# Reordering the end of layer 0's aggregation in a four-layer graph network: tail rows, T1's subtractions and one sum of quarters

## The chip, the cores and the metric

The kernel runs on one core of one Trainium2 chip. The metric is the device time of one execution in microseconds. Besides the timed runs there is one profiled execution, whose trace gives every instruction with its start, its length, its engine and what released it. All positions in the text below ("at 263.54") are microseconds from the start of that trace.

## The reference

`x` is 2708 x 512, `adj` is 2708 x 2708, all in float32. Four layers follow each other; each adds its result to `x`:

```
h = relu(layernorm(x))                                   # before every layer
layer 0: x += relu( dinv * ((adj + I) @ (dinv * h)) @ W0 )     # deg = adj.sum(1), dinv = (deg + 1) ** -0.5
layer 1: x += (dis * (adj @ (dis * h))) @ W1.T + b1            # dis = (deg + 1e-8) ** -0.5
layer 2: the form of layer 0 with W2
layer 3: x += sigmoid(attn_a * (softmax-like attention @ (h @ W_sa)) + attn_b * (adj @ (h @ W_g) + b_g))
```

In each layer the large piece is a product of `adj` (2708 x 2708) with 512 columns. The change concerns that product in layer 0 alone.

## The kernel before, in words

**Tiling.** The 2708 nodes are four quarters of 677. Of each quarter 640 rows (5 blocks of 128) go through the fast scheme below; the remaining 37 rows of each quarter are gathered in two "tail" row blocks (`NF` and `NF + 1`). The output of a product is kept transposed in `agg[128, 2, 2, 2, 2, 678]`: partition = feature within a block of 128, then half of the features, half of the output nodes, block in the half, quarter in the half, and the 677 columns of a quarter (one of padding), worked on in two halves `u` of 339 columns.

**Two levels of Strassen's scheme (Winograd's form).** A product is done as seven outer products (numbers 1 to 7) of sums of parts of `h` (`XA` to `XD`, formed in place in `h`) with sums of quarters of the adjacency (plain ones `y11`, `y12`, `y21`, `y22`, and sums `T1` to `T4`, kept in DRAM as `osum`). Each outer product is done for `u = 0` and `1`, and each of these is again seven inner products on TensorE: `inner_x` (L445) forms four sums of the features on VectorE, `inner_y` (L461) four sums of the four blocks `o11, o12, o21, o22` of the adjacency on VectorE (`t1` L468, `t2` L469, `t4` L470, `t3` L471, each 128 x 1695), and `multiply` (L486) runs the seven inner products in the fixed order `pa` (operand 1), `pb` (6, needs `t2`), `pa` again (2), `pc` (7, needs `t3`), `pd` (5, needs `t1`), `pc` again (4, needs `t4`), `pd` again (3). An inner product is 5 matmuls of 128 x 339 (10 records in the trace). The second use of a bank continues its sum, so VectorE must have read the first one: `u2` (L528) after `pb`, `u3` (L534) after `pc`, the writes to `agg` (L511 to L515) after `pd` and after the second `pc` and `pd`.

**Tail rows.** `tails` (L574) adds the 37-row remainders: for each quarter `q` and each `u` four matmuls over block `NF` (L549) and four short ones over `NF + 1` (L554), into four PSUM banks `pt`, of which three come from the same pool of five banks as `pa` to `pd`; each `pt` is added to `agg` by VectorE (L589). Their operand is loaded by `tail_rows` (L558): two transfers of 339 KB from `yt` on SyncE's queue, and two small VectorE additions for the self loops (L571).

**Order around the change.** In layer 0 `first_aggregate` (L629) runs the outer products 1 and 7 and then, for `u = 1` and then `u = 0`, the products 6, 2 and 4; then the tail rows of quarters 0 and 1; product 5 for `u = 0`, `1`; the tail rows of quarters 2 and 3; the epilogue of the first half of the nodes, `epilogue(H1)` (`next_x`, L832: projection `po` L822, relu on ScalarE L842, addition to `x` L847, layer norm); product 3; `epilogue(H2)`. In the iteration with `u = 0`:

- `t2u` holds the four blocks of T2. T4 = T2 + `y21` is formed into four other blocks (L767) and stored by GpSimd's queue; T1 = T2 - `y22` is formed in place, one block `k` at a time, by `third_less` (L770, subtraction at L775), each after a load of a block of `y22` on SyncE's queue into one of two buffers. These same two buffers then take the tail rows of quarters 0 and 1.
- The second half of T1 (`u = 1`) is made by transfers: `accumulated` (L662) loads `y12` on SyncE's queue and lets GpSimd's queue add `y11` to it during a transfer; then it is stored for later layers.
- `ends_of_sums` (L599) adds quarters of `agg` on VectorE: L600 adds `agg[:, 0, 1]` to `agg[:, 1, 1]`, L601 then adds `agg[:, 1, 1]` to `agg[:, 1, 0]`, 128 x 2712 each.
- `XB -= XD` (L784) and `XC += XA` (L794), 128 x 2560 each, prepare the products 5 and 3.

**Who orders the work.** Each engine executes its own queue. Where an instruction stands in it is decided when the program is built, by a scheduler with priorities from the order of the source; `with tc.issue_after(ins):` only places the instructions of its block behind `ins` in the queue of `ins`'s engine. `at_u2`, `at_u3`, `at_end` and the like are lists of instructions to refer to. Waits on data, buffers and banks are set automatically. An instruction that waits holds up everything behind it in its queue.

Of the kernel before, what the change touches and what calls it, by code (L numbers as in the profile page):

```python
# [1 line left out]

# [8 lines left out]
ALU = mybir.AluOpType  # L11
# [26 lines left out]
def gnn_kernel(  # L38
# [20 lines left out]
    nc = tc.nc  # L59
# [51 lines left out]
    agg = big.tile([P, 2, 2, 2, 2, U * W], FP, name="agg")  # L111
# [328 lines left out]
        nc.vector.scalar_tensor_tensor(o, a, -1.0, b, ALU.mult, ALU.subtract)  # L440


    at_v, at_u2, at_u3, at_end, at_shift = [], [], [], [], []

    def inner_x(X):  # L445
        n = half // 2
# [14 lines left out]
    def inner_y(blks, u, loops, t3=None):  # L461
        o11, o12, o21, o22 = blks
        if loops:
            add_loops(o11, u, loops)
            add_loops(o22, u, loops)
        t1, t2, t4 = (tpool.tile([P, KT, W], FP, tag="t", name=f"t{k}") for k in (1, 2, 4))
        t3 = o12 if t3 is None else t3
        nc.vector.tensor_add(t1, o12, o11)  # L468
        nc.vector.tensor_add(t2, o22, t1)  # L469
        nc.vector.tensor_add(t4, o21, t2)  # L470
        nc.vector.tensor_add(t3, o22, o12)  # L471
        return {1: o11, 2: o21, 3: o22, 4: t4, 5: t1, 6: t2, 7: t3}

    def outer_product(p, self_loops, *dests):
        X, key, times = OUTER[p]
        xs_ = inner_x(X)
        if key in PLAIN:
            loops = times if self_loops else 0
        else:
            loops = 0 if self_loops else -times  # L480
        for u in range(U):
            blks = [load_o(key, a, b, u) for a, b in QUAD]
            multiply(xs_, inner_y(blks, u, loops), u, dests)
            free.extend(blks)

    def multiply(xs_, ys, u, dests, beside=None):  # L486
# [4 lines left out]
        def product(ps, q, start):  # L491

            for k in range(KT):
                nc.tensor.matmul(  # L494
                    ps, xs_[q][:, k, :], ys[q][:, k, :],
                    start=start and k == 0, stop=k == KT - 1, skip_group_check=not start,
                )

        def bank(name):
            return ps_agg.tile([P, W], FP, tag="agg", name=name)  # L500
# [72 lines left out]

    def tails(self_loops, qs, loaded=None):  # L574

        for q in qs:
            blk, both = loaded[q] if loaded else tail_rows(self_loops, q)
            for u in range(U):
                tl = both[:, :, u]
                ps = [  # L580
                    (ps_agg if c < NC - 1 else ps_out).tile(
                        [P, W], FP, tag="agg" if c < NC - 1 else "out", name="pt"
                    )
                    for c in range(NC)
                ]
                tail_products(ps, tl, True)
                for c in range(NC):
                    d = agg[:, c // 2, q // 2, c % 2, q % 2, u * W : (u + 1) * W]
                    at_end.append(nc.vector.tensor_add(d, d, ps[c]).ins)  # L589
            free.append(blk)  # L590
# [38 lines left out]
    def first_aggregate(epilogue):  # L629
# [10 lines left out]
        t3 = {0: early[:2]}  # L640
# [32 lines left out]
        def keep_all(blks, key, u, a_b=QUAD):  # L673
            for a, b in a_b:
                keep_o(blks[QUAD.index((a, b))], key, a, b, u)


        t3 = {0: [free.pop(0), free.pop(0)] + t3[0], 1: blks[0]}
        came = {}
# [56 lines left out]
        for u in reversed(range(U)):  # L736
# [9 lines left out]
                    keep_all(t2u, "t2", u)  # L746
            multiply(xs_, ys, u, [(0, 1, "added")])
            u3_of_6 = at_u3[-1]
            if u == 1:
                with tc.issue_after(at_u2[-1]):  # L750
                    other_roots()
# [18 lines left out]
            def third_less(k, y, at):  # L770
                a, b = QUAD[k]
                if k > 0:
                    load_plain("y22", a, b, u, y)
                with tc.issue_after(at):
                    nc.vector.tensor_sub(t2u[k], t2u[k], y)  # L775

            if u == 1:
                free += [f for f in y21 if f is not early[2]]
                came = second_sums(QUAD[2:3])
            else:  # L780
                third_less(0, y22[0], at_u3[-1])
                third_less(2, y22[0], at_end[-1])
                with tc.issue_after(at_end[-1]):
                    nc.vector.tensor_sub(XB, XB, XD)  # L784
            xs_ = inner_x(XD)
            multiply(xs_, inner_y(t4, u, 0, own_t3), u, [(1, 0, "as it is")])
            if u == 1:
                free += t4
        third_less(1, y22[1], at_u2[-1])
        third_less(3, y22[1], at_end[-2])  # L790
        free += y22
        with tc.issue_after(at_end[-1]):
            rows = [tail_rows(True, q) for q in (0, 1)]
            nc.vector.tensor_add(XC, XC, XA)  # L794
        tails(True, (0, 1), rows)
        t1 = [t2u, [t4[3], more[2]] + [free.pop() for _ in range(2)][::-1]]
        assert not free
        came = accumulated({QUAD[k]: t1[1][k] for k in (0, 1, 3, 2)}, "y12", 1, "y11")
        ends_of_sums()
        xs_ = inner_x(XB)  # L800
        p5 = [(0, 1, "less"), (1, 1, "less")]
        for u in range(U):
            more_loops = OUTER[5][2] - (OUTER[6][2] if u == 0 else 0)
            if u == 1:
                with tc.issue_after(came):
                    keep_all(t1[u], "t1", u, QUAD[1:3])
            with tc.issue_after(at_end[-3]):
                ys = inner_y(t1[u], u, more_loops, own_t3 if u == 0 else None)
            keep_all(t1[u], "t1", u, QUAD if u == 0 else QUAD[::3])
            multiply(xs_, ys, u, p5)  # L810
        free += t2u + [f for f in t1[1] if f is not more[2]]
        tails(True, (2, 3))
        epilogue(H1)
        outer_product(3, True, (0, 1, "added"))
        epilogue(H2)


# [388 lines left out]
```

## Time and profile before

| | |
|---|---|
| median of 3 runs | 2152.69 us (2149.81 to 2153.11) |
| the profiled execution: its own time | 2146.91 us |
| its span in the trace | 2144.9 us (2.0 us lie around it) |
| TensorE matmuls busy | 2071.7 us of the span |
| VectorE busy | 1418.1 us |
| products 6, 2, 4 with `u = 0`: product 4's first matmul | at 250.19 |
| tails of quarters 0 and 1, first and last matmul | 258.75 to 297.2 |
| product 5, first to last matmul | 298.41 to 356.56 |
| tails of quarters 2 and 3 end, first matmul of `po` | 370.16 |
| epilogue H1 ends, product 3 begins | 404.60 |

The page has totals and 40 slices of the span; the other views are answers to questions about the trace: the timeline of an engine (start, length, engine, line, operation, what it writes and reads, count of records merged into the row, and in brackets the idle time ahead of it with what ended it), the busy time of the engines in given stretches, the waits, and the transfers with their time from issue to landing. Matmul ends in the trace are modelled and lie some 0.16 us after the start of the next.

### The profile page before, as it was taken

The numbers are of one execution on the slowest core, as the hardware profiler recorded it, in microseconds if no ns is written. First come the engines' busy times: TensorE is split into PE (matmuls) and PEld (weight loads), VectorE is DVE, ScalarE is ACT, GpSimd is POOL, SyncE is SP. The second block draws the span as 40 slices with busy tenths as digits, with TensorE's granted clock in tenths as the row PEclk, the third lists the DMA queues.
The fourth block names the chain that finished last, engine by engine and source line by source line (L and its number), as shares of the span: only waits on it lengthen the run. The fifth ranks groups of instructions, "written<-read, shape, count | busy, mean of one in ns | idle before, by whom it ended". The sixth has DMA issues, their size and how long they took to land.

```text
span 2144.9 us, 20028 instructions
## 1 busy us (share of the span) xinstructions
PE 2071.7 (97%) x7320; PEld 1289.3 (60%) x7320; DVE 1418.1 (66%) x2487; ACT 406.7 (19%) x826; POOL 180.9 (8%) x327
## 2 busy tenths in 40 slices
PE   5999988999999999999999999999999999999998
PEld 2566545556666645566664546666677666666664
DVE  3578857567676867776585969968537755666512
ACT  1330000221000010100002121000116534444401
POOL 0111010210000021100001130000001000000001
PEclk9999999999999999999999999999999999999999
DMA  9998484446554443654454556445541233233212
GB/s 370 295 363 254 165 271 172 164 142 207 177 172 162 156 163 132 230 177 157 164 171 138 202 191 218 169 156 159 189 168 71 96 101 106 88 101 99 81 40 65
DMA packets 78866, 359.47 MB, mean 168 GB/s; under 512 B 10556, under 2 KB 14524, under 8 KB 78640
## 3 DMA queue, kind: packets, MB, share of 16 engines
q1 hardware_dynamic: 50096, 245.43, 33.4%
q0 software_dynamic: 28672, 112.76, 16.2%
q8 instruction: 58, 0.95, 0.2%
q14 instruction: 40, 0.33, 0.0%
HBM read 294.61 MB, written 62.15 MB: 166 GB/s over the span
## 4 chain that ended last, share of the span: by engine, by line
PE 46%; issue 38%; DVE 7%; DMA 5%; POOL 3%; ACT 1%; POOLq 0%; SPq 0%; ACTq 0%; DVEq 0%
PE pa L494 10%; PE pc L494 10%; PE pd L494 9%; PE po L822 5%; PE pb L494 5%; DMA obuf<-in_yb_dram 3%; PE pg L961 3%; PE pt L549 2%; DMA ends<-xs 1%; POOL ends L829 1%; PE pt L554 1%; DVE ends L914 1%; POOL out_dram L1065 1%; POOL xs L848 1%; PE dg_ps L292 1%
## 5 line engine op out<-in xcount | busy, mean ns | idle before, releaser
L1113 PE MATMUL pe<-obuf,h 128*128 128x339 f32 x1280 | 372.8, 448 | 0.0
L494 PE MATMUL pa<-obuf,h 128*128 128x339 f32 x1040 | 318.6, 451 | 8.1 <-ACT h L223 4.1
L1113 PEld LDWEIGHTS pe<-obuf,h 128*128 128x128 f32 x1280 | 240.9, 189 | 126.6 <-issue 10.0
L822 PE MATMUL po<-ends,agg 128*128 128x512 f32 x640 | 281.4, 596 | 2.0 <-ACT ends L842 1.7
L494 PEld LDWEIGHTS pa<-obuf,h 128*128 128x128 f32 x1040 | 196.5, 190 | 114.5 <-issue 7.9
L822 PEld LDWEIGHTS po<-ends,agg 128*128 128x128 f32 x640 | 119.6, 190 | 144.8 <-issue 137.0
L494 PE MATMUL pc<-t,h 128*128 128x339 f32 x560 | 172.0, 454 | 11.6 <-DVE u L534 11.6
L494 PE MATMUL pb<-t,s 128*128 128x339 f32 x560 | 174.8, 459 | 3.6 <-DVE t L469 3.6
L1034 ACT ACTIVATE e<-r,nsr 128x339 f32<-128x339 f32 x352 | 170.7, 566 | 27.2 <-DVE obuf L1038 11.6
L522 ACT COPY v<-pa 128x339 f32<-128x339 f32 x56 | 24.7, 441 | 773.7 <-PE pa L494 757.2
L494 PE MATMUL pd<-t,s 128*128 128x339 f32 x560 | 169.2, 447 | 0.0
L494 PE MATMUL pd<-obuf,s 128*128 128x339 f32 x550 | 166.4, 448 | 1.3 <-DVE agg L511 1.3
L494 PEld LDWEIGHTS pc<-t,h 128*128 128x128 f32 x560 | 107.1, 192 | 68.0 <-DVE u L534 13.2
L494 PEld LDWEIGHTS pb<-t,s 128*128 128x128 f32 x560 | 108.4, 194 | 61.1 <-DVE t L469 5.3
L494 PEld LDWEIGHTS pd<-t,s 128*128 128x128 f32 x560 | 105.8, 189 | 54.4 <-issue 0.5
L494 PEld LDWEIGHTS pd<-obuf,s 128*128 128x128 f32 x550 | 104.0, 189 | 55.0 <-DVE agg L511 2.2
L494 PE MATMUL pc<-obuf,s 128*128 128x339 f32 x440 | 133.1, 448 | 0.0
L494 PEld LDWEIGHTS pc<-obuf,s 128*128 128x128 f32 x440 | 83.3, 189 | 42.7 <-issue 0.5
L469 DVE TENSOR_TENSOR t<-obuf,t 128x1695 f32<-128x1695 f32 x55 | 105.3, 1915 | 0.0
L848 POOL DMA_DIRECT2D xs<-ends x66 | 36.0, 545 | 801.8 <-DVE ends L847 750.5
L470 DVE TENSOR_TENSOR t<-obuf,t 128x1695 f32<-128x1695 f32 x52 | 99.5, 1913 | 0.5 <-PE pc L494 0.5
L1130 DVE COPY agg<-pe 128x339 f32<-128x339 f32 x16 | 7.5, 506 | 138.1 <-PE pe L554 138.1
(249 smaller groups left out, 2296.0 us busy)
## 6 DMA issues: line engine op xcount, KB each, us to landing
obuf<-in_yb_dram SPq DMA_DIRECT2D x132, 847.5 KB, 4.5
obuf<-osumt SPq DMA_DIRECT2D x100, 847.5 KB, 4.5
osumt<-obuf POOLq DMA_DIRECT2D x22, 847.5 KB, 9.6
xs<-ends POOLq DMA_DIRECT2D x66, 256.0 KB, 2.3
ends<-xs POOLq DMA_DIRECT2D x66, 256.0 KB, 3.5
obuf<-in_yt_dram SPq DMA_DIRECT2D x32, 339.0 KB, 3.6
obuf<-in_yb_dram POOLq DMA_DIRECT2D x11, 847.5 KB, 10.6
ends<-in_yb_dram SPq DMA_DIRECT2D x9, 847.5 KB, 8.9
```

The source lines that it names most:

```text
L292: nc.tensor.matmul(ps[g], first, y, start=n < 4, stop=n >= len(ops) - 4)
L469: nc.vector.tensor_add(t2, o22, t1)
L470: nc.vector.tensor_add(t4, o21, t2)
L494: nc.tensor.matmul(ps, xs_[q][:, k, :], ys[q][:, k, :], start=start and k == 0, stop=k == KT - 1, skip_group_check=not start,)
L522: at_v.append(nc.scalar.copy(v, pa).ins)
L549: nc.tensor.matmul(ps[c], h[:, NF, c * P : (c + 1) * P], tl[:, 0, :], start=start, stop=False)
L554: nc.tensor.matmul(ps[c], h[g, NF + 1, c * P : (c + 1) * P], tl[g, 1, :], start=False, stop=True)
L822: nc.tensor.matmul(po, cs[c], w_sb[:, c, :], start=(c == 0), stop=(c == NC - 1))
L848: nc.gpsimd.dma_start(xs[t], xt)
L961: nc.tensor.matmul(pk, cs[c], wg_sb[:, c, k, :], start=(c == 0), stop=(c == NC - 1))
L1034: nc.scalar.activation(e[:, k], row, AF.Exp, bias=nsr[:, t, s : s + 1], scale=1.0)
L1113: nc.tensor.matmul(pe[c], h[:, t, c * P : (c + 1) * P], a, start=(t == 0), stop=False)
```

## The change

All of it concerns layer 0; the other layers call `tails` and `outer_product` without the new arguments. It does the following:

1. `product` notes its last matmul in `at_pe`. `tails` places its matmuls behind the last one of the product traced before, where its rows were loaded ahead; the tail rows of quarters 2 and 3 are now loaded ahead too, their self-loop additions placed behind an entry of `at_end`.
2. T1's four subtractions (L775) are all placed behind the last sum (`t3`, noted in `at_y`) of product 4's `inner_y`, in the order 0, 1, 2, 3. Before, block 0 stood behind `u3` of product 2, block 2 behind its end, block 1 behind `u2` of product 4 and block 3 behind a later write. The sums of product 5's first half are placed behind the last subtraction, no longer behind a write of the tail rows.
3. `agg[:, 1, 1] += agg[:, 0, 1]` is no longer a VectorE addition (L600) but two accumulating transfers on GpSimd's queue, from `agg` to `agg`, 128 x 1356 each, traced after product 6 with `u = 0`. The second addition (L601) stays on VectorE, behind the end of the tail rows.
4. `XB -= XD` moves from product 2 with `u = 0` to product 4 with `u = 1`; `XC += XA` moves from the tail rows of quarters 0 and 1 to product 5 between its halves.
5. The sums for product 3 (`inner_x` and both `inner_y`) are placed behind the last addition of the tail rows of quarters 2 and 3.

```diff
--- before.py
+++ after.py
@@ -1,4 +1,4 @@
-from contextlib import ExitStack
+from contextlib import ExitStack, nullcontext
 
 import concourse.bass as bass
 import concourse.tile as tile
@@ -440,7 +440,7 @@
         nc.vector.scalar_tensor_tensor(o, a, -1.0, b, ALU.mult, ALU.subtract)
 
 
-    at_v, at_u2, at_u3, at_end, at_shift = [], [], [], [], []
+    at_v, at_u2, at_u3, at_end, at_shift, at_y, at_pe = [], [], [], [], [], [], []
 
     def inner_x(X):
         n = half // 2
@@ -468,19 +468,23 @@
         nc.vector.tensor_add(t1, o12, o11)
         nc.vector.tensor_add(t2, o22, t1)
         nc.vector.tensor_add(t4, o21, t2)
-        nc.vector.tensor_add(t3, o22, o12)
+        at_y.append(nc.vector.tensor_add(t3, o22, o12).ins)
         return {1: o11, 2: o21, 3: o22, 4: t4, 5: t1, 6: t2, 7: t3}
 
-    def outer_product(p, self_loops, *dests):
+    def outer_product(p, self_loops, *dests, at=None):
+
         X, key, times = OUTER[p]
-        xs_ = inner_x(X)
+        with tc.issue_after(at) if at is not None else nullcontext():
+            xs_ = inner_x(X)
         if key in PLAIN:
             loops = times if self_loops else 0
         else:
             loops = 0 if self_loops else -times
         for u in range(U):
             blks = [load_o(key, a, b, u) for a, b in QUAD]
-            multiply(xs_, inner_y(blks, u, loops), u, dests)
+            with tc.issue_after(at) if at is not None else nullcontext():
+                ys = inner_y(blks, u, loops)
+            multiply(xs_, ys, u, dests)
             free.extend(blks)
 
     def multiply(xs_, ys, u, dests, beside=None):
@@ -491,10 +495,11 @@
         def product(ps, q, start):
 
             for k in range(KT):
-                nc.tensor.matmul(
+                last = nc.tensor.matmul(
                     ps, xs_[q][:, k, :], ys[q][:, k, :],
                     start=start and k == 0, stop=k == KT - 1, skip_group_check=not start,
                 )
+            at_pe.append(last.ins)
 
         def bank(name):
             return ps_agg.tile([P, W], FP, tag="agg", name=name)
@@ -573,8 +578,10 @@
 
     def tails(self_loops, qs, loaded=None):
 
-        for q in qs:
-            blk, both = loaded[q] if loaded else tail_rows(self_loops, q)
+
+        at = at_pe[-1]
+        for n, q in enumerate(qs):
+            blk, both = loaded[n] if loaded else tail_rows(self_loops, q)
             for u in range(U):
                 tl = both[:, :, u]
                 ps = [
@@ -583,7 +590,8 @@
                     )
                     for c in range(NC)
                 ]
-                tail_products(ps, tl, True)
+                with tc.issue_after(at) if loaded else nullcontext():
+                    tail_products(ps, tl, True)
                 for c in range(NC):
                     d = agg[:, c // 2, q // 2, c % 2, q % 2, u * W : (u + 1) * W]
                     at_end.append(nc.vector.tensor_add(d, d, ps[c]).ins)
@@ -674,6 +682,11 @@
             for a, b in a_b:
                 keep_o(blks[QUAD.index((a, b))], key, a, b, u)
 
+        def accumulate(to, a):
+
+            for c in range(2):
+                nc.gpsimd.dma_start(to[:, c], a[:, c], accum_op=ALU.add)
+
 
         t3 = {0: [free.pop(0), free.pop(0)] + t3[0], 1: blks[0]}
         came = {}
@@ -746,6 +759,8 @@
                     keep_all(t2u, "t2", u)
             multiply(xs_, ys, u, [(0, 1, "added")])
             u3_of_6 = at_u3[-1]
+            if u == 0:
+                accumulate(agg[:, 1, 1], agg[:, 0, 1])
             if u == 1:
                 with tc.issue_after(at_u2[-1]):
                     other_roots()
@@ -772,31 +787,28 @@
                 if k > 0:
                     load_plain("y22", a, b, u, y)
                 with tc.issue_after(at):
-                    nc.vector.tensor_sub(t2u[k], t2u[k], y)
+                    return nc.vector.tensor_sub(t2u[k], t2u[k], y).ins
 
             if u == 1:
                 free += [f for f in y21 if f is not early[2]]
                 came = second_sums(QUAD[2:3])
-            else:
-                third_less(0, y22[0], at_u3[-1])
-                third_less(2, y22[0], at_end[-1])
-                with tc.issue_after(at_end[-1]):
-                    nc.vector.tensor_sub(XB, XB, XD)
             xs_ = inner_x(XD)
             multiply(xs_, inner_y(t4, u, 0, own_t3), u, [(1, 0, "as it is")])
             if u == 1:
                 free += t4
-        third_less(1, y22[1], at_u2[-1])
-        third_less(3, y22[1], at_end[-2])
+                with tc.issue_after(at_u3[-1]):
+                    nc.vector.tensor_sub(XB, XB, XD)
+        for k, y in ((0, y22[0]), (1, y22[1]), (2, y22[0]), (3, y22[1])):
+            minus_y22 = third_less(k, y, at_y[-1])
         free += y22
         with tc.issue_after(at_end[-1]):
             rows = [tail_rows(True, q) for q in (0, 1)]
-            nc.vector.tensor_add(XC, XC, XA)
         tails(True, (0, 1), rows)
         t1 = [t2u, [t4[3], more[2]] + [free.pop() for _ in range(2)][::-1]]
         assert not free
         came = accumulated({QUAD[k]: t1[1][k] for k in (0, 1, 3, 2)}, "y12", 1, "y11")
-        ends_of_sums()
+        with tc.issue_after(at_end[-1]):
+            nc.vector.tensor_add(agg[:, 1, 0], agg[:, 1, 0], agg[:, 1, 1])
         xs_ = inner_x(XB)
         p5 = [(0, 1, "less"), (1, 1, "less")]
         for u in range(U):
@@ -804,14 +816,20 @@
             if u == 1:
                 with tc.issue_after(came):
                     keep_all(t1[u], "t1", u, QUAD[1:3])
-            with tc.issue_after(at_end[-3]):
+            with tc.issue_after(minus_y22 if u == 0 else at_end[-3]):
                 ys = inner_y(t1[u], u, more_loops, own_t3 if u == 0 else None)
             keep_all(t1[u], "t1", u, QUAD if u == 0 else QUAD[::3])
             multiply(xs_, ys, u, p5)
+            if u == 0:
+                with tc.issue_after(at_end[-1]):
+                    nc.vector.tensor_add(XC, XC, XA)
         free += t2u + [f for f in t1[1] if f is not more[2]]
-        tails(True, (2, 3))
+        with tc.issue_after(at_end[-3]):
+            rows = [tail_rows(True, q) for q in (2, 3)]
+        tails(True, (2, 3), rows)
+        at = at_end[-1]
         epilogue(H1)
-        outer_product(3, True, (0, 1, "added"))
+        outer_product(3, True, (0, 1, "added"), at=at)
         epilogue(H2)
```

## The prediction, made before the changed kernel was run

> **What bounds the kernel now.** I read the page's totals and slices first, then busy time by stage, then the timelines of TensorE and VectorE where TensorE is not full.
>
> ```profile
> PE 2071.7 (97%) x7320; PEld 1289.3 (60%) x7320; DVE 1418.1 (66%) x2487; ACT 406.7 (19%) x826; POOL 180.9 (8%) x327
> PE   5999988999999999999999999999999999999998
> ```
>
> TensorE is busy 97% of the span; only the start and slices 5 and 6 (268 to 375 us) show it short of 9. By stage (product 4 begins, to the tails, to product 5, to its second half, to the epilogue, the epilogue):
>
> ```profile
> 250.00:258.75 8.75, 6.33 (x23) 3.64 (x21) 7.74 (x7) 0.89 (x2) 0.53 (x1) 1.00 0.76 255
> 258.75:298.40 39.65, 33.11 (x114) 18.63 (x114) 25.41 (x36) 0.00 (x0) 5.07 (x7) 0.87 0.76 226
> 298.40:335.80 37.40, 25.21 (x71) 15.26 (x72) 19.08 (x36) 0.44 (x1) 4.01 (x7) 0.82 0.72 238
> 335.80:370.20 34.40, 33.44 (x136) 19.93 (x134) 30.69 (x46) 0.45 (x1) 2.87 (x6) 1.00 0.61 208
> 370.20:404.80 34.60, 34.60 (x85) 15.46 (x82) 18.85 (x51) 11.24 (x18) 8.14 (x15) 1.00 0.39 138
> ```
>
> First number after the comma: TensorE busy; then weight loads, VectorE, ScalarE, GpSimd; near the end TensorE's granted clock. From 250 to 370.2 TensorE idles 120.2 - 98.1 = 22.1 us, and its clock falls to 0.87 and 0.82. The epilogue has no hole. TensorE's timeline names the holes:
>
> ```profile
> 258.75 0.81 PE L549 MATMUL pt<-obuf,h 128*128 128x339 f32 x2 [1.88 <-DMA obuf<-in_yt_dram]
> 261.73 1.50 PE L554 MATMUL pt<-obuf,h 32*128 32x339 f32 x2 [2.17 <-DMA obuf<-in_yt_dram]
> 263.54 5.18 PE L494 MATMUL pb<-t,s 128*128 128x339 f32 x10 [0.31 <-DVE t L469]
> ...
> 286.89 1.41 PE L549 MATMUL pt<-obuf,h 128*128 128x339 f32 x4 [2.06 <-DVE agg L589]
> ...
> 308.56 4.80 PE L494 MATMUL pb<-t,s 128*128 128x339 f32 x10 [3.32 <-DVE t L469]
> ...
> 327.41 5.66 PE L494 MATMUL pc<-t,h 128*128 128x339 f32 x10 [8.33 <-DVE u L534]
> ```
>
> A tail matmul put among product 4 waits for its rows, product 5's `pb` for its operand, `pc` for `u3`. An inner product normally shows 3.02 us, one each 2.86; after such holes it takes 5.18, 4.80, 5.66. VectorE's timeline says why `u3` was late:
>
> ```profile
> 280.51 1.93 DVE L775 TENSOR_TENSOR obuf<-obuf 128x1695 f32<-128x1695 f32 x1 [2.68 <-DMA obuf<-in_yb_dram]
> ...
> 299.47 2.98 DVE L601 TENSOR_TENSOR agg<-agg 128x2712 f32<-128x2712 f32 x1
> ...
> 320.09 0.19 DVE L571 TENSOR_TENSOR obuf<-obuf,ident 128x32 f32<-128x32 f32 x1 [8.92 <-DMA obuf<-in_yt_dram]
> ```
>
> A small self-loop addition waits for tail rows that product 5's end will need, with `u2` and `u3` queued behind it.
>
> **What could be had.** Without any stop the way from 250.19 is 21 inner products x 2.86 + 8 tail groups x 3.26 (366.90 to 370.16) + the epilogue's 34.4 = 120.6 us, to 370.8; it ends at 404.6. So 33.9 us lie there: 22.1 of holes and about 12 of slow restarts.
>
> **What the Trainium skill says.** "TensorE: Matmul & The Clock Gate", section Why this matters for your kernels: no idle gaps over some 3 us between matmul bursts, or the clock falls. The trace agrees: 0.53 us of idle costs 0.1, holes of 3.32 and 8.33 cost 1.8 and 2.6; but several near 2 us together cost as much (2.2 at 263.54). "Perfetto Trace Analysis", section Tensor Engine Instruction (MATMUL, LD_WEIGHTS): VectorE's, ScalarE's and GpSimd's queues are strictly first in, first out; the 8.92 above is that. "DMA: Bandwidth & Descriptors", section Queues, rings and completion order: a queue's transfers are consumed in ring order, and engines take turns between queues. In the trace a block of `y22` took 5.9 us from issue, 9.2 with GpSimd's w0 load, an accumulating transfer and a store beside it.
>
> **The change, part by part.** I place the new queue order on the old durations, from 250.19.
>
> *T1's subtractions behind product 4's sums, L600 gone.* VectorE loses 2.9 us at 233.4 and, ahead of product 4, two subtractions (1.84 each), `XB -= XD` (2.74) and a load's wait (1.01). Its sums for product 4 end: `t2` 253.5, `t4` 255.7, `t3` 257.6. `pb` starts at 253.5, 0.5 after `pa`; before, 263.54. Two subtractions then fit before `u3` (needed 262.4). The third needs `y22(1,0)`, loadable only when the first has freed its buffer (259.8); with the w0 load beside it I take 6.6 us (5.9 to 9.2 to 11): 266.4, subtraction to 268.4. Behind it in VectorE's queue stands the write of `pd` to `agg`, which the second `pd` (due 267.8) waits for: **1.0 us** lost. Product 4 ends at 271.7 instead of 279.98.
>
> *Tails behind product 4.* The hole at 258.75 to 263.5 goes. The rows of quarter 0 take the buffer of the third subtraction; issued at 268.5 behind the last `y22` block on SyncE's queue, they land at about 273.5: **2.0 us**. The rows of quarter 1 follow the fourth subtraction (its block in by 272, done 274) and land about 280. Their self-loop addition stands in VectorE's queue ahead of the first evictions of `pt`, which begin at 280.2, when `t2` and `t3` of product 5 follow (1.83 each), and `t4` after the next four. With five banks the second group stops for 2.6, the third 2.3, the fourth 0.4 us: **5.3**, plus one slow restart **1.9**. Product 5 starts at 271.7 + 2.0 + 13.05 + 5.3 + 1.9 = 294 (before 298.41), but with all its operands ready: the holes of 3.32 and 8.33 and their slow restarts go.
>
> *The sum by transfers.* GpSimd issues both at 231 to 234, where its queue is idle until 238.97. Nearest rows: an accumulating load of 847.5 KB took 8.7 to 10.8 us, a plain `agg` to `agg` copy of twice the size 12.5 us. I take 9 each (bounds 5 and 25): in by 250, needed by L601's successor at 296. T4's stores behind them (4.0 to 4.9 each) slip a few us, wanted only at 259 and later. Nothing is gained or lost here beyond VectorE's 2.9 us above, since TensorE reads no part of it before the epilogue; landing after 296 would cost its lateness one for one.
>
> *T1's second half, and the queues.* On SyncE's queue the first `y12` block (into a buffer free at 257.6) now stands ahead of `y22(1,0)`; it costs it about 0.7 us, within the 6.6. On GpSimd's, the store of T1's block moves from ahead of the w0 load to behind it; only later layers read it. The other `y12` loads on SyncE's queue stand behind a tail-row load that waits for `t3` (285.6). From there: load 6, accumulate 9, a store's issue 0.6, the last accumulating transfer 9.4: near 311. VectorE wants it at 19.2 us into product 5 = 313. Just hidden; beyond that, one for one.
>
> *`XC += XA` between product 5's halves.* 2.8 us ahead of `t4` and `t3` of the second half. `t3` follows `t2` by 0.85 + 2.8 + 1.83 + 1.83 = 7.3, while TensorE has `pb` and four fifths of `pa`, 5.15: stop 2.2, slow restart 1.9, and `pb` 0.5: **4.6**. The moved `XB -= XD` falls at 201.5 into 2.4 us of VectorE idle time: nothing, below 0.5 if that cover is short. Tails of quarters 2, 3: no sums among their evictions, **0.3**.
>
> *Product 3's sums behind the tails.* Before, they lay beside product 5. Now 12.1 us (four feature sums of 0.74, nine loop additions of 0.2, four block sums of 1.83) lie between the epilogue's first additions to `x`. I followed VectorE, ScalarE and the `x` loads (4.2 us, behind the layer norms that free their places): the first three normalizations end 6.7 us later than before, the relu of the eighth tile is queued behind the next three on ScalarE, and two `po` banks leave TensorE 0.4 and 4.2 us idle, slow restart 1.9: **6.5** (0 to 8).
>
> **Sum.** Lost: 0.5 + 1.0 + 2.0 + 5.3 + 1.9 + 4.6 + 0.3 + 6.5 = 22.1 of 33.9: the gain is 11.8 us. After 404.6 the order is the same and TensorE full, so it stays to the end: the profiled execution goes from 2146.91 to 2135.1. That execution is 5.8 below the median; on the median, 2152.69 - 11.8 = **2140.9**.
>
> **Rivals.** About 0.2% (4.3 us) is what a measurement can tell from no change here.
>
> *Most is had (10%).* The epilogue's chain doesn't close (6.5 back), evictions are half as late (about 3.5 back): gain 22, 2131. For: the epilogue before has 13.7 us of VectorE idle ahead of its additions. Against: the ScalarE order above.
>
> *The moved waits take the place (14%).* `y22(1,0)` lands after 9.2 to 11 us, so product 4 stops 4 to 5 us and restarts slowly (+2), and the tail rows follow that: gain about 4, at most 6, 2149. For: the 9.2 measured under the same traffic. Against: the accumulating transfer then lies behind w0, not beside it.
>
> *The addition doesn't come off, or is hidden elsewhere (3%).* No change, 2152: only if the scheduler's order didn't hold; the built order shows it.
>
> *Slower (8%).* The chain of T1's second half slips: load, accumulation and a store issued before the last accumulation, one after another. From 313 each us is one us; to end over 4.3 us slower it must land 16 us late, at 329. With the worst rows (9.7, 10.8, 10.8) it lands at 318; it takes waiting behind stores, one of which took 12.5, at two places: 2158.
>
> *As forecast (65%)*: gains of 6 to 18, 2135 to 2147.
>
> **Numbers.** Bounds: `y22` and tail rows -1 to +6, evictions -3 to +2, the epilogue -6.5 to +1.5, the sum by transfers 0; the range 2130 to 2150 is gains of 2.7 to 22.7 and leaves out the slower case, no change and a sliver of the others, some 15%. Faster by over 0.2%: 65 + 10 + a third of 14, 0.80; within 0.12; slower 0.08.
>
> **What would show it.** Right: product 4's `pb` near 253.5, the second sum of quarters before 297 without waiting, no wait on `yt` ahead of `u3`, the second `pd` of product 4 and the second tail group waiting for VectorE, `pc` in product 5's second half waiting for `t3`, `po` waiting for ScalarE. Wrong: a full epilogue, a wait for the sum's transfers, or product 5's second half waiting for accumulated blocks.

## The result, and the profile after

The changed kernel takes 2135.9 us (median of 6 runs, 2133.05 to 2141.1); the kernel before, run beside it, 2150.53 us. The ratio is 0.9934, with a 95% interval of 0.9917 to 0.995, so the gain is 11 to 18 us. The profiled execution takes 2133.39 us instead of 2146.91 (span 2131.5 instead of 2144.9). The forecast was 2140.9, and 11.8 us for the profiled execution.

The page of the changed kernel, the totals and TensorE's slices:

```profile
PE 2064.2 (97%) x7320; PEld 1285.7 (60%) x7320; DVE 1413.2 (66%) x2486; ACT 406.0 (19%) x826; POOL 182.4 (9%) x329
PE   5999989999999999999999999999999999999997
```

Counted from 0, slice 6 (320 to 373 us) is full now, slice 5 still isn't. TensorE's busy time fell by 7.5 us for the same 7320 matmuls, 5.3 of them between product 2 and product 3 with `u = 0`, where its granted clock rose from 0.93 to 0.97. Two stretches of the changed kernel (first number after the comma TensorE's busy time, near the end its granted clock and the DMA share):

```profile
258.75:288.80 30.05, 21.91 (x77) 12.56 (x75) 18.26 (x28) 0.44 (x1) 3.80 (x6) 0.89 0.96 342
288.80:328.90 40.10, 34.81 (x126) 21.05 (x123) 26.58 (x39) 0.88 (x2) 5.96 (x9) 0.97 0.94 296
```

The first, the end of product 4 with most of the tail rows behind it, still has TensorE idle for 8.1 of 30.05 us. Its timeline names the stops that are left:

```profile
254.11 3.13 PE L498 MATMUL pb<-t,s 128*128 128x339 f32 x10 [0.40 <-DVE t L469]
...
269.45 3.12 PE L498 MATMUL pd<-obuf,s 128*128 128x339 f32 x10 [0.79 <-DVE agg L516]
277.21 4.76 PE L554 MATMUL pt<-obuf,h 128*128 128x339 f32 x8 [4.63 <-DMA obuf<-in_yt_dram]
...
286.81 1.41 PE L554 MATMUL pt<-obuf,h 128*128 128x339 f32 x4 [2.72 <-DVE agg L597]
...
292.15 1.41 PE L554 MATMUL pt<-obuf,h 128*128 128x339 f32 x4 [1.81 <-DVE agg L597]
...
325.21 4.81 PE L498 MATMUL pb<-t,s 128*128 128x339 f32 x10 [2.95 <-DVE t L469]
...
389.52 3.70 PE L840 MATMUL po<-ends,agg 128*128 128x512 f32 x8 [1.42 <-ACT ends L860]
```

Product 4 stops only for 0.40 and 0.79 us and ends at 272.6 (before at 280.1); then TensorE waits for the rows of quarter 0, and twice for VectorE to read a bank `pt` (an eviction). Product 5 has no stop in its first half; in the second, `pb` waits. The stop of 8.33 us is gone. Two of the stops are followed by a slow restart, that is, by matmuls that take longer than normal: 4.76 us for eight records at 277.21 (normally 2.45), 4.81 for ten at 325.21 (normally 3.02). From here on three segments count: product 4's first matmul to product 5's, from there to the first `po`, and from there to product 3's first matmul (H1). Each ratio is to the kernel before, run beside that version.

| kernel | median us | ratio to before, 95% interval | product 4 to 5 | product 5 to `po` | H1 | product 2 to 3 |
|---|---|---|---|---|---|---|
| before | 2150.5 | | 48.22 | 71.75 | 34.44 | 174.42 |
| changed | 2135.9 | 0.9934 [0.9917, 0.995] | 47.08 | 59.17 | 36.12 | 162.37 |
| e1, subtractions back | 2134.5 | 0.9938 [0.9923, 0.9952] | 46.43 | 59.96 | 36.09 | 162.49 |
| e2, rows of quarters 2, 3 back | 2136.6 | 0.9944 [0.9926, 0.9961] | 46.19 | 61.27 | 36.16 | 163.62 |
| e3, product 3's sums back | 2132.3 | 0.9926 [0.991, 0.9942] | 46.31 | 59.71 | 34.44 | 160.47 |
| e4, `XC += XA` back | 2134.6 | 0.9938 [0.9923, 0.9953] | 46.91 | 57.94 | 36.09 | 160.94 |
| e5, sum on VectorE back | 2136.5 | 0.9942 [0.9928, 0.9957] | 46.68 | 59.39 | 36.07 | 162.15 |
| e6, sum by transfers alone | 2147.8 | 0.9997 [0.9987, 1.0006] | 48.79 | 72.10 | 34.44 | 175.33 |
| e7, tails placed freely | 2137.6 | 0.9944 [0.9927, 0.9961] | 46.18 | 59.85 | 36.15 | 162.18 |
| e8, own places for rows | 2124.8 | 0.9886 [0.987, 0.9903] | 39.17 | 57.28 | 36.11 | 152.56 |
| e9, product 5's sums back | 2133.1 | 0.9925 [0.991, 0.994] | 42.78 | 63.07 | 36.20 | 162.05 |
| e10, e9 and e2 together | 2145.9 | 0.9979 [0.9971, 0.9986] | 43.36 | 73.87 | 36.07 | 173.30 |
| e11, product 5's sums alone | 2136.2 | 0.9939 [0.9922, 0.9955] | 47.74 | 62.81 | 34.44 | 164.99 |
| e12, e8 and e3 together | 2125.9 | 0.9893 [0.9879, 0.9908] | 38.60 | 62.10 | 34.44 | 155.15 |

The last column runs from product 2's first matmul to product 3's, so it contains everything that was touched but `XB -= XD`, which now lies at 201.95. The span less that column is 1970.5 before, 1969.1 changed, and 1967.1 to 1973.4 over all fourteen profiled executions, though the rest of the program is the same: differences of up to 6 us outside the stage are not the change's. So 12.05 of the 13.4 us between the two spans are accounted for by the stage; the 1.4 left lie within that spread. One trace stands behind each row. The edits of e2, e3 and e7 leave product 4 and the first tail rows as the change made them, and yet these take 46.18 to 47.08 us in the four: differences under 1 us say nothing.

### The profile page after: what moved, and what is told of

The parts are those of the page before. It is cut to its first block, busy times and chain, and to the rows that moved or that the text cites. A ratio compares the mean times of both kernels' runs of the same rounds, so it can differ in the third digit from the quotient of the medians.

```text
span 2131.5 us, 20035 instructions
## 1 busy us (share of the span) xinstructions
PE 2064.2 (97%) x7320; PEld 1285.7 (60%) x7320; DVE 1413.2 (66%) x2486; ACT 406.0 (19%) x826; POOL 182.4 (9%) x329
## 4 chain that ended last, share of the span: by engine, by line
issue 45%; PE 39%; DMA 6%; DVE 5%; POOL 3%; ACT 0%; POOLq 0%; SPq 0%; ACTq 0%; DVEq 0%
PE pa L498 9%; PE pc L498 9%; PE pd L498 9%; PE pb L498 5%; PE po L840 4%; DMA obuf<-in_yb_dram 3%; PE pt L554 2%; DMA ends<-xs 1%; PE pg L979 1%; POOL ends L847 1%; POOL xs L866 1%; DVE ends L932 1%; DMA obuf<-in_yt_dram 1%; POOL out_dram L1083 1%; DMA xs<-ends 1%
```

## The experiments

Each of e1 to e5, e7 and e9 is the changed kernel with one part undone; e6 and e11 are the kernel before with one part alone. "Stage" is the last column of the table.

**e1: T1's subtractions back.**

```
+            else:
+                third_less(0, y22[0], at_u3[-1])
+                third_less(2, y22[0], at_end[-1])
...
-        for k, y in ((0, y22[0]), (1, y22[1]), (2, y22[0]), (3, y22[1])):
-            minus_y22 = third_less(k, y, at_y[-1])
+        third_less(1, y22[1], at_u2[-1])
+        minus_y22 = third_less(3, y22[1], at_end[-2])
```

> The changed kernel with one part undone: the four subtractions that make T1 stand in VectorE's queue where they stood before (two of them ahead of product 4's operands), the rest as changed. Measured by the stage from product 2's first matmul to product 3's first matmul, 174.4 us before and 162.4 changed. Theory (the gain comes from the subtractions and the tail rows' place together): product 4's first inner products get their operands later again by the two subtractions and the wait in front of the second (1.84 x 2 + 1.0), now with no tail matmul between them, and the fourth's rows come earlier: product 4 stops 4 to 6 us at pb or pc, the tails' wait for the rows shrinks; stage 164 to 169. Rival (the gain is the sum by transfers' 2.9 us and the moves of XC and XB): the stage stays within 1 us of 162.4.

Stage 162.49, 0.12 more: the rival's number, by the theory's mechanism. TensorE's timeline:

```profile
262.38 4.73 PE L498 MATMUL pb<-t,s 128*128 128x339 f32 x10 [4.00 <-DVE t L469]
278.38 2.44 PE L554 MATMUL pt<-obuf,h 128*128 128x339 f32 x8
```

`pb` stops 4.00 us again, with a slow restart, as expected. But the tail rows, asked for earlier (256.85 instead of 269.00), are there when product 4 ends, and the 4.63 us are gone. Product 4's stop and the wait for the rows stand for each other: whichever comes first, product 5 begins 46 to 47 us after product 4.

**e2: the rows of quarters 2 and 3 back.**

```
-        with tc.issue_after(at_end[-3]):
-            rows = [tail_rows(True, q) for q in (2, 3)]
-        tails(True, (2, 3), rows)
+        tails(True, (2, 3))
```

> The changed kernel with one part undone: the rows of quarters 2 and 3 are not loaded and added to ahead of the tails, but in the tails as before, so that the scheduler may put their small self-loop additions early in VectorE's queue. Theory: the small addition stands again ahead of product 5's u2 and u3 and waits for its rows some 9 us; pc stops again, the stage grows from 162.4 to 170 to 174. Rival (subtractions alone made the gain): the addition waits beside cover, the stage stays below 165.

Stage 163.62: the theory missed, the rival's number came (not its reason: e1 took the subtractions away and lost nothing). The small additions do stand among product 5's first half again, but the rows are there early enough (the longest wait is 4.2 us, and it stops no matmul of that half). So something else made the rows come early; e9 to e11 find it.

**e3: product 3's sums back.**

```
-        outer_product(3, True, (0, 1, "added"), at=at)
+        outer_product(3, True, (0, 1, "added"))
```

> The changed kernel with one part undone: product 3's sums on VectorE are free to lie beside product 5 again, instead of behind the tails, among the epilogue's additions. Theory of the prediction: the epilogue, 36.1 us from its first matmul to product 3's with the sums in it and 34.4 before, returns to 34.4, so the stage would be 160.7 if the sums cost nothing beside product 5. Rival (the sums are worth more behind the tails: beside product 5 they sit ahead of operands or of evictions of pt): the epilogue returns to 34.4, but product 5 or its tails stop by 3 to 12 us, stage 164 to 172.

H1 is 34.44 again and the stage 160.47: the theory. In this kernel's timeline the epilogue's 80 matmul records run without a stop:

```profile
356.98 34.60 PE L840 MATMUL po<-ends,agg 128*128 128x512 f32 x80
```

So the sums cost 1.7 us where the change put them, and beside product 5 no more than 0.5 (59.71 for 59.17).

**e4: `XC += XA` back.**

```
             rows = [tail_rows(True, q) for q in (0, 1)]
+            nc.vector.tensor_add(XC, XC, XA)
...
-            if u == 0:
-                with tc.issue_after(at_end[-1]):
-                    nc.vector.tensor_add(XC, XC, XA)
```

> The changed kernel with one part undone: XC += XA lies among the tails of quarters 0 and 1 again instead of between product 5's halves. Theory of the prediction: t3 of product 5's second half then comes 2.8 us earlier, the pc stop goes (it was only 0.16), the tails' evictions are later by up to 2.8 with their own stops 2.72 and 1.81 growing; the second half's pb stop stays at 2.95, because it comes from the accumulated transfer and not from this addition: stage 162 to 165. Rival (the 2.95 us at pb comes from this addition in VectorE's queue): the pb stop falls to 0.5, the stage to 158 to 160.

Stage 160.94: just below the theory's 162, and above the rival's 158 to 160. The stop at `pb` is 2.15 instead of 2.95, not 0.5, so most of it isn't the addition's. Counted from product 4's first matmul, the last accumulated block came 1.0 us sooner than in the changed kernel; why was not taken apart. Between product 5's halves the addition costs 0.16 us, the stop of `pc`.

**e5 and e6: the sum of quarters on VectorE again, and by transfers alone in the kernel before.**

```
-                accumulate(agg[:, 1, 1], agg[:, 0, 1])
+                nc.vector.tensor_add(agg[:, 1, 1], agg[:, 1, 1], agg[:, 0, 1])
```

> The changed kernel with one part undone: the first half of the sum of agg's quarters is an addition on VectorE again (2.9 us), not two accumulating transfers. Theory: the addition lies behind product 6's last evictions, ahead of T1's and product 4's sums or in an idle stretch of VectorE; product 4's pb comes 0 to 2.9 us later and so the stage 162.4 to 165.3. Rival 1 (the sum by transfers made the gain): stage 170 to 174. Rival 2 (the two accumulating transfers hold up loads on the DMA engines): the stage falls below 162 and the y22 and yt loads land over 1 us earlier.

> The kernel before with one part of the change alone: the first half of the sum of agg's quarters by two accumulating transfers, and the second addition at the place of the old two. Theory: in the kernel before the addition stood ahead of product 4's operands among two subtractions and XB's; the stage from product 2's first matmul to product 3's falls from 174.4 by 0 to 2.9. Rival (the transfers made the gain): it falls to about 162.

162.15, and 175.33 where before had 174.42: within 1 us both ways, and e6's ratio is 0.9997 [0.9987, 1.0006]. The 2.9 us that VectorE saves ahead of product 4 don't bring its `pb` forward: in e6 the first tail matmul ahead of it waits 3.36 us for its rows, where it waited 1.88 before. The transfers of the changed kernel, with KB and median time to landing:

```profile
agg<-agg POOLq DMA_DIRECT2D x2, 678.0 KB, 6.1
```

**e7: tails placed freely.**

```
-                with tc.issue_after(at) if loaded else nullcontext():
-                    tail_products(ps, tl, True)
+                tail_products(ps, tl, True)
```

> The changed kernel with one part undone: the tails' matmuls are not placed behind the product they follow, so the scheduler may put a group among product 4 or 5. Theory: a group of tail matmuls stands ahead of product 4's last inner products and waits for the rows of quarter 0, which land no earlier than 277; the same wait (4.63) falls earlier and is longer by what stands behind it, up to 9 us: stage 163 to 171. Rival (the scheduler keeps the groups behind the product anyway with the new VectorE order): no change of order, stage 162.4 within 1.

162.18, the rival: with the rest of the change the scheduler puts none of quarter 0's or 1's groups among product 4 anyway. Some of quarter 2's stand among product 5's second half again, as before.

**e8: what the remaining stops are worth.** Two blocks of their own for quarter 0's rows, loaded early; the additions for quarter 1's rows behind the first group's evictions; `y12` in the order 0, 1, 2, 3; the loads for quarters 2 and 3 behind the last `y12` load; `XC += XA` behind `u3` of product 5's second half.

```
+    def own_rows(q):
+        apart = [left[:, 0 : U * W].rearrange("p (u w) -> p u w", u=U),
+                 ytp.tile([P, 2, W], FP, tag="yt", name="tl")]
...
-            rows = [tail_rows(True, q) for q in (0, 1)]
+            rows = [tail_rows(True, 0, rows0)]
...
-        came = accumulated({QUAD[k]: t1[1][k] for k in (0, 1, 3, 2)}, "y12", 1, "y11")
+        came = accumulated({QUAD[k]: t1[1][k] for k in (0, 1, 2, 3)}, "y12", 1, "y11")
...
-        with tc.issue_after(at_end[-3]):
+        with tc.issue_after(at_end[-3]), tc.issue_after(at_load[-1]):
             rows = [tail_rows(True, q) for q in (2, 3)]
```

> A version meant to take what the changed kernel still loses, by the theory that its remaining stops come from the buffer of quarter 0's rows, the order of the rows' additions and the last accumulated block. The rows of quarter 0 are loaded early into places of their own; the rows of quarter 1 are added to behind the first group's evictions; the y12 blocks come in the order 0, 1, 2, 3; the loads for the rows of quarters 2 and 3 stand behind the last y12 load; XC += XA follows product 5's second half. Theory: the stops of 4.63 (first pt), 2.72 and 1.81 (later pt) and 2.95 (pb of the second half), 12.1 us with their slow restarts near 16, mostly go: stage 150 to 156, 6 to 12 us faster than the changed kernel. Rival (the transfers are the bound, DMA share .94 to .96 in these stages, so an earlier load only makes another later): stage above 160.

Stage 152.56, 9.8 us less than the changed kernel, and 2124.8 us, the fastest version here (its interval and the changed kernel's don't meet). TensorE's timeline of e8:

```profile
273.25 2.44 PE L555 MATMUL pt<-ends,h 128*128 128x339 f32 x8
...
280.08 2.63 PE L555 MATMUL pt<-ends,h 128*128 128x339 f32 x4 [1.66 <-DVE agg L616]
...
317.20 4.81 PE L498 MATMUL pb<-t,s 128*128 128x339 f32 x10 [1.49 <-DVE t L469]
```

The first tail group starts with no wait. The DMA engines were 94 to 96% busy in these stages of the changed kernel, yet no other transfer came late enough to take the gain back.

**e9: product 5's first-half sums back.** This part had not been undone in any of the eight.

```
-            with tc.issue_after(minus_y22 if u == 0 else at_end[-3]):
+            with tc.issue_after(at_end[-3]):
```

> After eight runs no single part undone brings the time back, so a part that none of them touched must carry the gain, or two parts do the same. New theory: it is the edit that lets product 5's first-half sums, with the self-loop additions of T1 ahead of them, follow the last subtraction instead of the tails' evictions. The stores of T1 follow those additions (at 274 us changed, 305 before) and free the buffers for the rows of quarters 2 and 3. Here that edit alone is undone in the changed kernel; the rows' additions stay behind product 5. Theory: pb of product 5's first half stops about 3 us and restarts slowly (2), the stores go at 302 or later and the rows of quarters 2 and 3 land past 318, but nothing of product 5 stands behind them; the tails may wait; the evictions of the first tail groups come earlier (2.72 and 1.81 go, up to 4.5): stage 161 to 167. Rival (the gain lies in the tails and subtractions): the stage stays within 1 us of 162.4.

162.05, which both would give, but the segments differ: product 4 to 5 is 4.3 us shorter than in the changed kernel, product 5 to `po` 3.9 longer. TensorE's timeline:

```profile
277.71 4.86 PE L554 MATMUL pt<-obuf,h 128*128 128x339 f32 x8 [5.01 <-DMA obuf<-in_yt_dram]
294.65 3.18 PE L498 MATMUL pa<-obuf,h 128*128 128x339 f32 x10 [1.20 <-DVE obuf L430]
...
304.80 5.93 PE L498 MATMUL pb<-t,s 128*128 128x339 f32 x10 [3.32 <-DVE t L469]
```

Without the sums among their evictions the tail groups behind the first don't stop at all; the 3.32 us of before is back at `pb`.

**e10: e9 and e2 together.**

> The changed kernel with two parts undone together: product 5's first-half sums follow the tails' evictions as before, and the rows of quarters 2 and 3 are loaded and added to wherever the scheduler puts them. Theory (the two do the same work): the small self-loop addition stands ahead of u3 again and waits for rows that the late stores hold back, 8 to 9 us; pc stops about 8, stage 168 to 175. Rival: stage within 2 us of 162.4, the gain is in neither.

173.30, the theory. This is the whole stage of before but for 1.1 us, with the subtractions, the tails and the sum by transfers as changed. The chain can be read from the timelines of e10. GpSimd's queue:

```profile
296.28 0.88 POOL L678 DMA_DIRECT2D obuf<-in_yb_dram  x1 [9.86 <-DMA obuf<-in_yb_dram]
...
304.10 1.08 POOL L418 DMA_DIRECT2D osumt<-obuf  x2 [6.38 <-DMA obuf<-in_yb_dram]
```

The trace doesn't name the blocks; by the order of the source and by what is waited for, the first row accumulates a block of T1's second half, and the first of the two stores keeps that block, once it has landed. The second store, at 304.65, is one of T1's first half: its self-loop addition had ended at 294.8, but it stands behind the other two. It lands 7.3 us later, and SyncE loads rows into the buffer that it read:

```profile
312.08 4.55 SPq L568 DMA_DIRECT2D obuf<-in_yt_dram  x4
```

VectorE's small addition waits for these rows, `u3` behind it (the row at 297.65 is T1's other self-loop addition):

```profile
297.65 0.64 DVE L430 SCALAR_TENSOR_TENSOR obuf<-ident,obuf 128x128 f32<-128x128 f32 x3
...
319.43 0.19 DVE L576 TENSOR_TENSOR obuf<-obuf,ident 128x32 f32<-128x32 f32 x1 [12.97 <-DMA obuf<-in_yt_dram]
```

and TensorE for `u3`:

```profile
324.01 5.80 PE L498 MATMUL pc<-t,h 128*128 128x339 f32 x10 [11.32 <-DVE u L539]
```

The stop is 11.32 here and was 8.33 before. TensorE was ready for this `pc` 6.4 us sooner than in the kernel before (product 5 began 4.7 us sooner, and `pb` had no slow restart), but the rows came at nearly the same time (319.4 for 320.1), so that `pc` began only 3.4 us sooner: nearly half of what had been gained is handed back here. In the kernel before, one more wait stood between the rows and `u3` (VectorE of before):

```profile
326.29 0.65 DVE L430 SCALAR_TENSOR_TENSOR obuf<-ident,obuf 128x128 f32<-128x128 f32 x3 [1.44 <-DMA obuf<-in_yb_dram]
```

This is the self-loop addition of product 3's first block, which SyncE had asked for at 315.71. It held `u3` back by some 1.9 us more (an estimate: in e10 `u3` starts 0.61 us behind `u2`, there 2.53). Placing product 3's sums behind the tails takes it away; no run tests that part of the stop alone.

In the changed kernel T1's self-loop additions stand right behind the subtractions (VectorE),

```profile
273.54 1.20 DVE L430 SCALAR_TENSOR_TENSOR obuf<-ident,obuf 128x128 f32<-128x128 f32 x6
```

the stores follow, now ahead of the accumulating transfers in GpSimd's queue,

```profile
274.48 1.09 POOL L418 DMA_DIRECT2D osumt<-obuf  x2 [4.67 <-DVE obuf L430]
```

and the first rows of quarter 2 are asked for at 291.70 and not at 312 (SyncE):

```profile
291.70 0.33 SPq L568 DMA_DIRECT2D obuf<-in_yt_dram  x1
```

**e11: product 5's first-half sums alone, in the kernel before.**

```
-        third_less(3, y22[1], at_end[-2])
+        minus_y22 = third_less(3, y22[1], at_end[-2])
...
-            with tc.issue_after(at_end[-3]):
+            with tc.issue_after(minus_y22 if u == 0 else at_end[-3]):
```

> The kernel before with one edit alone: product 5's first-half sums may follow the last of the four subtractions instead of the tails' evictions. Nothing else of the change is in it. Theory: the self-loop additions of T1 come by 285 us, the stores right behind, the rows of quarters 2 and 3 land before 312; the stops of 3.32 (pb) and 8.33 (pc) and their slow restarts (1.8 and 2.6) go, product 4's own holes (4.4 us and a slow restart) stay, product 3's sums still lie beside product 5: stage from 174.4 to 160 to 165, as fast as the changed kernel. Rival (the tails, the subtractions and the sum are needed too): stage above 169.

164.99, just within the theory's 160 to 165: one edit gives 9.4 of the 12.05 us, and whole executions can't be told from the changed kernel's (ratios 0.9939 and 0.9934, with intervals that overlap). Its mechanism holds in part. The stop of 3.32 is gone, but `pc` still stops, since the rows of quarter 3 keep their small addition ahead of `u3` (TensorE, then VectorE of e11):

```profile
319.08 5.26 PE L494 MATMUL pc<-t,h 128*128 128x339 f32 x10 [5.90 <-DVE u L534]
```

```profile
316.65 0.19 DVE L571 TENSOR_TENSOR obuf<-obuf,ident 128x32 f32<-128x32 f32 x1 [10.09 <-DMA obuf<-in_yt_dram]
```

**e12: e8 with product 3's sums free** (the edits of e8 and e3).

> The version with own places for quarter 0's rows (stage 152.6), and product 3's sums free to lie beside product 5 again, which made the epilogue 34.4 instead of 36.1 us in the changed kernel. Theory: both add up, stage 150 to 151.5. Rival (beside product 5 the sums now stand ahead of its evictions or operands, since it runs sooner): a stop of over 1 us in product 5 or its tails takes it back, stage 152 to 155.

155.15, the rival's side and 0.15 past its 155: H1 is 34.44, but a stop of 3.47 comes at product 5's `pd` (TensorE),

```profile
312.49 6.01 PE L498 MATMUL pd<-obuf,s 128*128 128x339 f32 x10 [3.47 <-DVE s L511]
```

behind a self-loop addition that waits 7.52 us for its block (VectorE),

```profile
311.37 0.65 DVE L430 SCALAR_TENSOR_TENSOR obuf<-ident,obuf 128x128 f32<-128x128 f32 x3 [7.52 <-DMA obuf<-in_yb_dram]
```

It is product 3's: its first piece has 128 columns, where those of T1's second half have 45, and the block was asked for at 300.48 by line 412, which loads for an outer product; the accumulated blocks are loaded by line 422. So one of the freed sums itself holds up the reading of `pd`, as the rival has it. In e3 the same addition waited 4.58 us without stopping TensorE; in the kernel before it was the last to release `u3`. The two gains don't add.

## Why the prediction was right, and which of its terms were not

The sum holds: 11.8 us forecast, 12.05 measured in the stage. Its parts do so only together, so that it came this close is luck. By segment, the forecast was 4.4 gained from product 4 to 5, 13.9 from product 5 to `po`, 6.5 lost in H1. Measured: 1.1, 12.6 and 1.7. The first two came out 4.6 us worse in sum, the third 4.8 better.

- **T1's subtractions.** The step is right: `pb` stops 0.40 (0.5), the second `pd` 0.79 behind the third subtraction's write (1.0), product 4 ends at 272.6 (271.7, with a start 0.5 us earlier). But e1 shows that it is worth nothing that can be told from zero (0.12 us): the time is spent waiting for tail rows. The prediction counted that wait at 2.0; it was 4.63.
- **Rows of quarter 0: mis-sized.** They were issued at 269.0, as put (268.5), but landed at 277, not 273.5, with the DMA engines 96% busy. The wait was 4.63 for 2.0, and the slow restart that the sum had put at the evictions (1.9) came here: eight records in 4.76 us where 2.45 is normal, 2.3. e8 loads these rows early into places of their own, and the segment falls by 7.9 us, some of it from its other edits.
- **Evictions of `pt`: right.** Two stops, 2.72 and 1.81, for 5.3 in three, with no slow restart behind them. e9 takes the sums away from among the evictions: both stops go and the segment is 4.3 us shorter, against 7.2 with its slow restart in the sum.
- **The stops in product 5's first half go: right, and the gain.** It rested on the operands standing ready and on the small additions no longer standing ahead of `u3`. What the prediction did not see is that in the changed kernel these are two guards for the stop at `pc`: with either left in place the stage stays at 162.05 (e9) or 163.62 (e2), and without both it is 173.30 (e10). Nor did it say that the early self-loop additions make the early stores, and these the early loads. Its reading of the stop was short, too: the last to release `u3` before was not the rows' addition but product 3's, shown at e10.
- **Product 5's second half: size right, cause wrong.** 4.6 was put, 0.5 of it at `pb` and the rest at `pc`, because of `XC += XA`. It lost 2.95 at `pb` and 1.8 in a slow restart, because the last accumulated block of T1 was late. VectorE of the changed kernel:

```profile
320.46 0.61 DVE L430 SCALAR_TENSOR_TENSOR obuf<-ident,obuf 128x45 f32<-128x45 f32 x3 [3.25 <-DMA obuf<-in_yb_dram]
```

  The step that failed is "just hidden": the block was put near 311 and came near 320. The row load ahead of the `y12` load on SyncE's queue waited for `t3`, ready at 291.7 and not at 285.6, 6.1 us later; the transfers behind it took the rest. The prediction had named a wait of this half for accumulated blocks as a sign of being wrong, and 318 as the latest landing with the worst rows. As the prediction said, beyond its due time each us of lateness costs one; product 5 began 3.8 later than put, so only 2.95 showed. `t3` does follow `t2` by 7.25 us (7.3), but the slow restart stretched `pb` and `pa` to 7.1 us, which covers it but for 0.16.
- **The sum by transfers: right.** 6.1 us each (9 put), no effect in e5 or e6.
- **Tails of quarters 2 and 3: right.** No stop (0.3 put).
- **Product 3's sums in H1: mis-sized.** 6.5 put (0 to 8), 1.7 measured by e3. One `po` bank stopped, 1.42; the other stop of 4.2 us and its slow restart did not come. Which step of that chain was shorter than put was not taken apart.

Of the rivals, "the moved waits take the place" comes near what happened from product 4 to 5, and only there (1.1 us gained of 4.4 forecast), but not for its reason: `y22(1,0)` was not late (its subtraction began at 267.05, put at 266.4), the rows of quarter 0 were. "Slower" names the chain of T1's second half; that chain did slip, but by too little to outweigh the gain. That the transfers of the sum made the gain is refuted by e6; that transfers bound this stretch anyway, by e8.

## What to carry to other kernels

A stop at an in-order queue can have several causes in parallel: undo parts in pairs as well as singly before saying which one made the gain, since here seven single undoings cost at most 1.3 us and one pair 10.9. Follow a late load back through its buffer: the store that frees it, the instruction the store waits for, and that one's place in its own queue. A product that ends earlier is worth only what the next fixed arrival allows (here product 4 took 8.1 us less, and product 5 followed 1.1 us sooner), so price the loads that follow it under the traffic of that moment.

## What the hardware showed that was not expected

In these runs the cost of a slow restart does not follow from the length of the stop alone. In e9 and e10 the same last four stops precede `pb` (5.0, 1.20, 0.53 and 3.32 us; e10 had one of 0.76 ahead of them), and the inner product took 5.93 us in one and 3.12 in the other. The stretch behind it, of e9 and then of e10, with the granted clock third from the end:

```profile
304.80:308.00 3.20, 3.20 (x6) 2.06 (x7) 2.62 (x3) 0.00 (x0) 1.99 (x4) 0.50 0.90 353
```

```profile
303.80:307.00 3.20, 3.15 (x11) 2.19 (x12) 2.67 (x3) 0.00 (x0) 2.51 (x4) 1.00 0.92 367
```

And in e8 a stop of only 1.49 us, with one of 0.53 shortly before it, was followed by an inner product of 4.81. So the sentence of the Trainium skill drawn on above ("TensorE: Matmul & The Clock Gate", section Why this matters for your kernels), that gaps over some 3 us lower the clock, holds here as a tendency: a shorter one did it, and one of 3.32 did not. What decides stays open. A term for slow restarts is thus uncertain by about 2.8 us a stop.
